# Four stacked graph-attention layers: the row of attention terms R moved by transfers instead of transposes, and a retuned list order

## The chip, the core and the metric

The kernel runs on one core of one Trainium2 chip. Time is device microseconds of one execution; a run's time is the median of several. The core has five engines that work side by side: PE (TensorE, matmuls and transposes, with PEld for its weight loads), DVE (VectorE), ACT (ScalarE), POOL (GpSimd) and SP (SyncE, which here only issues DMAs). Each engine takes its instructions in a fixed order and waits at an instruction until what it needs is there.

## What is computed

Input x has 32 batches of 512 nodes with 256 features, adj is a 512 x 512 adjacency of about 3% ones. Four layers follow one another, each on `h = relu(layernorm(x))`, each added to x:

```python
# layer 0 (layer 1 is the same with slope 0.01, relu at the end)
Wh = h @ W
e = leaky_relu((Wh @ a1)[:, :, None] + (Wh @ a2)[:, None, :], 0.2)
e = where((adj > 0) | eye(N), e, -inf)
x = x + elu(softmax(e, -1) @ Wh)
# layer 2: the same with 4 heads of 64 features
# layer 3
out = relu(h @ mlp1_w + mlp1_b)                      # 512 features
out = elu(gat(out, None, W_fc, a_fc)) + out          # attention without a mask
out = relu(out @ mlp2_w + mlp2_b)                    # 256 features
out = elu(gat(out, adj, W_hand, a_hand)) + out       # attention with the mask
x = x + relu(out)
```

All of it is in 32-bit floats.

## The kernel before

**How an attention is done.** With p the source term and q the target term of a node, exp(leaky_relu(p + q)) is a maximum of two products, so after dividing by a factor of the target row, the weight of node j for node i is `max(R[i], T[j]) * mask[j, i]` times a factor of j that is put on the values. `values` (L669) makes the tile v: for each of four tiles of 128 nodes a matmul of hT with the weights W, to which three more columns were added (W times the vectors a, with the slopes in them); ACT takes the exponential of these three columns into v[:, t, F:F+3] and scales the values by the first. `weights` (L704) makes `wt`, [j on partitions, four tiles j, 512 nodes i]: DVE's `scalar_tensor_tensor` (L714) takes the maximum of R (512 wide, the same on every partition) with a column T of v, times `maskT`. `averages` (L756) then runs the four matmuls of `wt` with v for one tile of nodes; column F of the result is the sum by which it is divided.

**Where R comes from.** R has to stand on all 128 partitions. In `weights` without `r`, PE transposes the column v[:, t, F+2], broadcast to 128 x 128, four times into a PSUM bank, and DVE reads it there. This is the way of layer 0, layer 1 and the last attention of layer 3, which all go through `plain` (L749). Layer 2 and `sort_attend` have another: `rows_out` (L721) transposes the columns once into 4 (or 16) rows of 128, ACT copies them into the SBUF tile `row` (one buffer), a DMA on SP writes them to a line in DRAM (four buffers), and `spread` (L731) reads that line back with a DMA that repeats it on 128 partitions, into a tile with three buffers.

**Streams.** Four streams each carry every fourth batch through all layers, one behind the other by LEAD. The layers are generators; each `yield after_us(t)` says when this stream goes on: the start of its last piece, plus STRETCH times the matmul time of it, plus SLOW times t. The main loop at the end of `fast` always goes on with the stream that is due first. This settles the order in which instructions are written down, and that place is their rank.

**The list scheduler.** The program is built twice. In the first pass `jobs_of` (L165) collects which instruction needs which, `price` (L110) gives each a time, and `in_order` (L251) plays them through: each engine takes, of the instructions that are ready, the one with the lowest rank. For a DMA, `price` has a landing time by kind (`spread` 4.3 us, `row` 2.6). The order of each engine and the PSUM bank of each tile are kept, and in the second pass `arrange` (L388) ties the instructions of each engine into this order. The times in `price`, LEAD, SLOW, STRETCH and the pauses thus appear in no instruction; they settle the order alone. SP's DMAs are in it as well: an SP instruction that waits for a transfer holds all that stand behind it.

**The beginning.** All loads are issued by SP in one list: two vectors for W0, x of batch 0, W0, adj, x of batches 1 to 3, then the other weights, vectors and biases. `setup` (L568), run beside the first streams with the banks of the fourth, makes the mask: DVE turns adj into ones and zeros (`own`), POOL's `affine_select` (L572) sets the diagonal to one, PE transposes it in 16 blocks, ACT copies the blocks as `maskT`. After that it finishes the weights of the later layers (`finish_w`, L498: transposes and small matmuls, POOL for the vectors, DVE for the columns) and the constants `before`, `after` and `band` for the sort.

**`sort_attend`** (L956) replaces the unmasked attention for all batches but the last: POOL scatters the rows in the order of their terms into DRAM (`order`), SP brings them back (`sums`), prefix sums are made, SP writes them as `table`, and POOL gathers from it (`g`). It stays as it is but for its pauses.

If a value is too large or adj has a case that this scheme doesn't cover, `general` computes everything again; it doesn't run with these inputs.

Of the kernel before, what the change touches and what calls it, by code (L numbers as in the profile page):

```python
# [30 lines left out]
P = 128  # L31
# [36 lines left out]
class Job:  # L68

    def __init__(self, place, ins):  # L70
        self.place, self.ins = place, ins
        self.engine, self.op = str(ins.engine).split(".")[-1], ins.opcode
        self.real, self.soft = set(), set()
        self.after, self.behind, self.opens, self.uses = [], [], [], set()
        self.ready, self.left, self.led, self.rank = 0.0, 0, False, place
# [34 lines left out]
def price(job, outs, ins, in_psum):  # L110

    e, op = job.engine, job.op
    if op == "Matmult":
        (name, _, moving), (_, _, still) = ins[0], ins[1]
        job.span = int(job.ins.tile_size[1])
        turned = name.startswith("ident")
        whole = str(list(job.ins.ins)[1].dtype).endswith("float32")
        job.passes = 2 if whole and not turned else 1
        job.rest, job.fills = [], outs[0][0]
        job.load = 109.0 * elements(still) / P * job.span / P  # L120
        job.flow = 109.0 if turned else (elements(moving) * (5.0 / 6.0 if whole else 0.45) + 2.4) * job.span / P
        return
    n = max(elements(s) for _, _, s in outs + ins) if outs + ins else 1
    wide = [name for name, _, s in ins if elements(s) > 48]
    columns = sum(1 for _, _, s in ins if elements(s) == 1) if n > 48 else 0
    if op == "DMACopy":
        name, _, s = outs[0]
        kind = name.split("_")[0].rstrip("0123456789")
        large = elements(s) * s[0][1] > 5000
        job.took = LANDING.get(kind, 6000.0) if large else SHORT.get(kind, 3300.0)  # L130
        if kind == "spread":
            job.took += 900.0 * (ins[0][1] // 512)
        if kind == "x" and ins[0][1] == 0:
            job.took = 5000.0
        job.holds = (2000.0 if kind == "order" else 1290.0) if e == "Pool" else 600.0 if kind in ("sums", "table") else 400.0
        return
    if e == "DVE":
        if op == "BNStats":
            t = 409.0
        elif n <= 48:  # L140
            t = 158.0 + n
        elif op in ("TensorTensor", "TensorReduce") or len(wide) > 1:
            t = 155.0 + 1.042 * n + (55.0 * columns if op == "TensorScalarPtr" else 0.0)
        elif any(map(in_psum, wide)):
            t = 205.0 + 1.045 * n
        else:
            t = 205.0 + 0.43 * n + 45.0 * columns
        job.holds = max(45.0, t - 84.0)
    elif e == "Activation":
        if n <= 48:  # L150
            t = 170.0 + n + 90.0 * (len(ins) > 1)
        elif any(map(in_psum, wide)):
            t = 170.0 + 0.82 * n + 90.0 * min(columns, 1)
        else:
            t = 200.0 + 0.84 * n + 85.0 * min(columns, 1)
        job.holds = max(60.0, t - 100.0)
    else:
        t = 1271.0 if op == "TensorTensor" and n > 48 else 250.0
        job.holds = t
    if len(outs) > 1:  # L160
        job.holds, t = job.holds + 85.0, t + 165.0
    job.took = t
# [88 lines left out]
def in_order(jobs, users, homes):  # L251
# [27 lines left out]
    array = {"load": 0.0, "flow": 0.0, "end": 0.0, "span": P, "idle": 0.0, "last": 0.0}  # L279
# [23 lines left out]
    def put(job, e, at):  # L303
# [21 lines left out]
        else:  # L325
            clock[e], done = at + job.holds, at + job.took
        array["last"] = max(array["last"], done)
# [71 lines left out]
def fast(ctx, tc, plan, flag, x, adj, w0, a0, w1, a1, w2, a2, mlp1_w, mlp1_b, mlp2_w, mlp2_b,  # L399
# [10 lines left out]
    LEAD = 75.63  # L410
    SLOW = 1.43
    STRETCH = 1.5
# [98 lines left out]
    a0_sb = fetch_a(a0, "W0a")  # L511
    xts = {0: load_x(0)}
    W0, _ = fetched0 = fetch_w(w0, a0_sb, "W0")
# [54 lines left out]
    def setup():  # L568
# [3 lines left out]
        nc.gpsimd.affine_select(  # L572
            out=own, in_=own, pattern=[[P, NT], [-1, N]], base=0, channel_multiplier=1,
            compare_op=OP.not_equal, fill=1.0,
        )
        nc.vector.tensor_reduce(differ[:, 0:1], adj_sb, AX.XY, OP.min)
        nc.vector.tensor_scalar(differ[:, 0:1], differ[:, 0:1], 0.0, None, op0=OP.is_lt)
        for j in range(NT):
            p = bank()
            for t in range(NT):  # L580
                transpose(p[:, t * P:(t + 1) * P], own[:, t, j * P:(j + 1) * P], ident)
            nc.scalar.copy(maskT[:, j, :], p)
        yield
# [69 lines left out]
    def turned(xn, when):  # L653
# [5 lines left out]
        yield after_us(2.12)  # L659
# [9 lines left out]
    def values(hT, w, rs=None):  # L669

        v = work.tile([P, NT, F + 3], FP, tag="v", name="v", bufs=4)
        for t in range(NT):
# [14 lines left out]
            if t + 1 < NT:  # L687
                yield after_us(0.72)
        yield after_us(0.03)
        return v  # L690

    def linear_t(inT, w, bias, name, bufs):
# [3 lines left out]
        for f in range(ft):  # L696
# [4 lines left out]
            yield after_us(0.76 if f == ft - 1 else 1.59)  # L701
# [47 lines left out]
    def plain(hT, w, rs=None):  # L749
        v = yield from values(hT, w, rs)  # L750
        wt = weights(lambda t: v[:, t, F + 2:F + 3], lambda j: v[:, j, F + 1:F + 2])
        note(v[:, :, F:])
        yield after_us(4.32)
# [19 lines left out]
    def layer0(xt, xn, rs, when):  # L773
        v, wt = yield from plain((yield from turned(xn, when)), W0)
        xn, rs = new_xn(), small([NT], "rs")
        for t0 in range(0, NT, 2):
            r, q = pair(), pair("q")
            for i in range(2):
# [3 lines left out]
                if i == 0:  # L782
                    yield after_us(2.78)
            add_elu(xt[:, t0:t0 + 2, :], r, q)
            norm(xt, xn, rs, t0, True)
            last, when = when, after_us(1.15)
            if t0 == 0:
                yield after_us(5.01)
# [3 lines left out]
    def layer1(xt, xn, rs, when):  # L792
        v, wt = yield from plain((yield from turned(xn, when)), W1, rs)
        xn, rs = new_xn(), small([NT], "rs")
        for t0 in range(0, NT, 2):
            r = pair()
            for i in range(2):
                p, rd = averages(v, wt, t0 + i)
                nc.scalar.activation(r[:, i, :], p, AF.Relu, scale=rd)
                if i == 0:  # L800
                    yield after_us(2.38)
# [3 lines left out]
            last, when = when, after_us(4.67)  # L805
            if t0 == 0:
                yield after_us(12.63)
# [3 lines left out]
    def layer2(xt, xn, rs, when):  # L811
        hT = yield from turned(xn, when)
        v = work.tile([P, NT, NH, CH], FP, tag="v", name="v2", bufs=4)
        for t in range(NT):
# [11 lines left out]
            yield after_us(0.87 if t + 1 < NT else 0.62)  # L826
# [4 lines left out]
        def begin():  # L831
# [4 lines left out]
            return after_us(1.36)  # L836
# [7 lines left out]
        yield after_us(9.98)  # L844
        begin()
        note(v.rearrange("p t h c -> p (t h) c")[:, :, D:])
        yield after_us(7.5)
        when = begin()
        for g, parts in enumerate(plan):
# [10 lines left out]
            yield after_us(0.16)  # L860
# [29 lines left out]
            yield after_us(0.3)  # L890
# [3 lines left out]
        yield after_us(9.4)  # L894
        return xn, rs, after_us(1.32)
# [28 lines left out]
    def attend(oT, b):  # L924

        halves, ends = fc_values()
        for c in range(2):
            for t in range(NT):
                project_half(oT, halves, ends, c, t)
                yield after_us(0.3)  # L930
# [4 lines left out]
        yield after_us(0)  # L935
        ys = []
        for t in range(NT):
# [10 lines left out]
            yield after_us(0.16)  # L948
            if t:
                mlp_in(oT, ys[t - 1], t - 1)  # L950
                yield after_us(0.3)
        yield after_us(3.15)
        mlp_in(oT, ys[-1], NT - 1)
        yield after_us(2.72)

    def sort_attend(oT, b):  # L956
# [6 lines left out]
        for t in range(NT):  # L963
            project_half(oT, halves, ends, 0, t)
            yield after_us(0.49)
        project_half(oT, halves, ends, 1, 0)
        yield after_us(0.06)
# [3 lines left out]
        yield after_us(0.73)  # L971
# [10 lines left out]
        sort = after_us(16.48)  # L982
        yield after_us(7.62)
        for t in range(1, NT):
            project_half(oT, halves, ends, 1, t)
            yield after_us(1.52)
# [7 lines left out]
        for c in range(2):  # L994
# [17 lines left out]
            sort = after_us(1.66)  # L1012
        places = table[:N, :].rearrange("(p t) (k c n) -> p (t k) c n", t=NT, k=2, c=2)
        sort = after_us(6.05)
        for c in range(2):
# [15 lines left out]
            yield after_us(3.52)  # L1031
# [14 lines left out]
            sort = after_us(1.5)  # L1046
        yield after_us(4.72)
# [12 lines left out]
        landed = after_us(9.21)  # L1060
        for t in range(NT):
# [13 lines left out]
            landed = after_us(2.51)  # L1075
            when.append(after_us(1.17))
# [6 lines left out]
        yield after_us(0)  # L1083

    def layer3(xt, xn, when, b):
# [3 lines left out]
        v, wt = yield from plain(rT, WHA)  # L1089

        n = 1 if b == B - 1 else 2
        for t0 in range(0, NT, n):
            y, q = pair()[:, :n, :], pair("q")[:, :n, :]
            for i in range(n):
# [3 lines left out]
                yield after_us(1.72)  # L1098
# [40 lines left out]
    def batch(b):  # L1139
        if b < NS:  # L1140
            first_norm(b)
            yield after_us(1.86)
        else:
            yield after_us(3.78)
        xt, xn, rs = normed.pop(b)
        when = after_us(4.88)
        for layer in (layer0, layer1, layer2):
            xn, rs, when = yield from layer(xt, xn, rs, when)
        if b + NS < B:
# [11 lines left out]
    ready = {i: i * LEAD + late for i, late in enumerate((0, -2.47, -0.73, -8.03))}  # L1161
    streams = [stream(i) for i in range(NS)]
    early = setup()
    ready[NS] = 0.35
    while ready:
        i = min(ready, key=ready.get)
        if i == NS:
            turn[0] = NS - 1
            ready[i] += 1.5
# [464 lines left out]
```

## Time and profile before

| | |
|---|---|
| median of 5 runs | 2784.59 us (2782.7 to 2785.1) |
| the profiled execution | 2785.95 us, from first to last instruction 2784.0 |
| mean granted TensorE clock | 0.995 |
| DMA bytes | 287.37 MB, 103 GB/s in the mean |
| DMA issues: spread, row, `sums`, `table`, out, x | 159, 63, 124, 62 + 62, 66, 32 on SP |
| DMA issues on POOL: `order`, `g` | 248, 124 |

PE's busy time is the union of its matmuls with modelled ends, so two matmuls in a row overlap by a little; the distance between their starts (the pitch) says how long each holds the array. fp32 matmuls run in two passes and count as two instructions in the trace.

### The profile page before, as it was taken

What the parts mean: (1) busy time and instruction counts of PE and PEld (TensorE: products, weight loads), DVE (VectorE), ACT (ScalarE), POOL (GpSimd) and SP (SyncE); (2) the same over time, 40 slices, a digit from 0 to 9 for tenths busy, and PEclk for the clock granted to TensorE, in tenths of its full rate; (3) what the DMA queues carried; (4) which work ended last, traced back from release to release, by engine and by line L of the source; (5) the groups of instructions that cost most, each with busy time, mean ns of one, the idle gap of its engine ahead of it and who ended that gap; (6) DMA issues with size and microseconds to landing.
All of it is one profiled execution on the core that took longest, in us unless ns stands there. A gap on an engine that the chain in (4) does not pass through costs nothing.

```text
span 2784.0 us, 41668 instructions
## 1 busy us (share of the span) xinstructions
PE 2739.4 (98%) x14316; PEld 1953.8 (70%) x14316; DVE 2272.9 (82%) x5834; ACT 1634.0 (59%) x4142; POOL 517.3 (19%) x515
## 2 busy tenths in 40 slices
PE   6999999999999999999999999999999999999997
PEld 6676686767776677766866667776686766867665
DVE  4779887897978879788796888978888898888964
ACT  3455666566655666556655566655666556655555
POOL 0012221122202222022211222111221122211220
PEclk9999999999999999999999999999999999999999
DMA  3024342343413433134331433223432233422430
GB/s 99 16 80 134 103 144 63 104 130 103 149 46 115 134 111 130 35 124 128 115 118 50 134 121 124 92 69 115 130 117 90 84 127 111 140 74 88 136 113 32
DMA packets 202499, 287.37 MB, mean 103 GB/s; under 512 B 18156, under 2 KB 157350, under 8 KB 202280
## 3 DMA queue, kind: packets, MB, share of 16 engines
q1 hardware_dynamic: 172520, 186.34, 21.5%
q0 software_dynamic: 29760, 98.30, 10.6%
q8 instruction: 114, 1.87, 0.3%
q14 instruction: 105, 0.86, 0.1%
HBM read 169.14 MB, written 115.45 MB: 102 GB/s over the span
## 4 chain that ended last, share of the span: by engine, by line
PE 92%; DVE 4%; ACT 1%; DMA 1%; issue 1%; SPq 0%; POOL 0%; POOLq 0%; ACTq 0%
PE b L430 70%; PE b L434 12%; PE b L438 10%; DVE w L714 1%; DVE st L630 0%; DVE y L771 0%; DMA W<-in_L_gnn_W_dram 0%; DVE xn L637 0%; DVE y L1107 0%; DMA spread<-row 0%; DVE y L764 0%; DMA g<-table,at 0%; DMA WHAa<-in_L_gnn_a_hand_dram 0%; DMA row<-row 0%; ACT q L780 0%
## 5 line engine op out<-in xcount | busy, mean ns | idle before, releaser
L430 PE MATMUL b<-v,w 128*128 128x257 f32 (+1 forms) x3136 | 766.0, 382 | 2.0 <-DVE w L718 1.0
L430 PEld LDWEIGHTS b<-v,w 128*128 128x128 f32 x3136 | 572.9, 191 | 122.1 <-issue 34.2
L430 PE MATMUL b<-WFC,oT 128*128 128x256 f32 (+1 forms) x2048 | 490.6, 381 | 1.5 <-ACT oT L700 1.5
L430 PEld LDWEIGHTS b<-WFC,oT 128*128 128x128 f32 x2048 | 374.4, 189 | 75.4 <-issue 18.6
L430 PE MATMUL b<-W,hT 128*128 128x259 f32 (+1 forms) x1536 | 396.0, 388 | 0.5 <-ACT hT L651 0.5
L714 DVE SCALAR_TENSOR_TENSOR w<-spread,v,maskT 128x512 f32<-128x512 f32 x512 | 373.5, 779 | 13.9 <-PE b L434 13.1
L434 PE MATMUL b<-w,v 128*32 128x512 f32 x3072 | 349.4, 595 | 0.0
L998 POOL DMA_INDIRECT order<-v,at x248 | 262.1, 1057 | 410.3 <-DVE at L980 147.0
L430 PEld LDWEIGHTS b<-W,hT 128*128 128x128 f32 x1536 | 279.0, 192 | 61.1 <-issue 22.7
L714 DVE SCALAR_TENSOR_TENSOR w<-b,v,maskT 128x512 f32<-128x512 f32 x384 | 264.7, 743 | 22.6 <-PE b L438 20.3
L1110 POOL TENSOR_TENSOR x<-x,y 128x512 f32<-128x512 f32 x62 | 81.8, 1320 | 1036.4 <-ACT y L1108 1027.1
L430 PE MATMUL b<-hT,WM 128*128 128x512 f32 x512 | 243.7, 592 | 0.4 <-ACT hT L651 0.4
L1052 POOL DMA_INDIRECT g<-table,at x124 | 137.1, 1106 | 568.0 <-DVE rden L746 180.2
L434 PEld LDWEIGHTS b<-w,v 128*32 128x32 f32 x3072 | 89.9, 109 | 198.1 <-issue 195.5
L430 PE MATMUL b<-oT,WM 128*128 128x512 f32 x512 | 227.5, 593 | 0.0
L630 DVE BATCH_NORM_STATS2 st<-x 128x6 f32<-128x256 f32 x512 | 194.4, 408 | 5.1 <-DMA x<-in_x_dram 3.7
L651 ACT ACTIVATE hT<-b 128x512 f32<-128x512 f32 x256 | 147.4, 593 | 45.6 <-PE b L438 45.6
L430 PEld LDWEIGHTS b<-oT,WM 128*128 128x128 f32 x512 | 97.2, 190 | 102.7 <-issue 99.9
L746 DVE RECIPROCAL rden<-b 128x1 f32<-128x1 f32 x388 | 57.8, 160 | 136.2 <-PE b L430 133.5
L438 PE MATMUL b<-ident,xn 128*128 128x128 f32 x1024 | 158.5, 276 | 8.2 <-DVE xn L637 8.2
L771 DVE TENSOR_TENSOR y<-q,y 128x512 f32<-128x512 f32 (+1 forms) x194 | 132.6, 683 | 33.8 <-ACT q L770 33.5
L922 ACT ACTIVATE v<-b,ends 128x256 f32<-128x256 f32 x256 | 120.4, 470 | 63.2 <-PE b L430 50.2
(154 smaller groups left out, 4236.6 us busy)
## 6 DMA issues: line engine op xcount, KB each, us to landing
table<-sums SPq DMA_DIRECT2D x62, 1032.0 KB
spread<-row SPq DMA_DIRECT2D x159, 256.0 KB
sums<-order SPq DMA_DIRECT2D x62, 516.0 KB
x<-in_x_dram SPq DMA_DIRECT2D x32, 512.0 KB
out_dram<-x SPq DMA_DIRECT2D x62, 256.0 KB
sums<-order SPq DMA_DIRECT2D x62, 129.0 KB
order<-v,at POOLq DMA_INDIRECT x248, 2.7
g<-table,at POOLq DMA_INDIRECT x124, 5.0
```

The costliest lines, as they stand in the source:

```text
L430: nc.tensor.matmul(p, w, x, **flags)
L434: nc.tensor.matmul(p, w, x, tile_position=(0, c), **flags)
L438: nc.tensor.transpose(p, x, i)
L630: nc.vector.bn_stats(st[:, i, :], xt[:, t0 + i, :])
L651: nc.scalar.activation(hT[:, :, t0 * P:(t0 + 2) * P], p.rearrange("p (k n) -> p k n", k=KF), AF.Relu)
L714: nc.vector.scalar_tensor_tensor(wt[:, j, :], r, t_col(j), maskT[:, j, :], op0=OP.max, op1=OP.mult)
L746: nc.vector.reciprocal(r, den)
L771: nc.vector.tensor_tensor(r, q, r, op=OP.add)
L922: nc.scalar.activation(halves[c][:, t, :F], ps[:, :F], AF.Copy, scale=ends[:, t, 0:1])
L998: one = nc.gpsimd.indirect_dma_start(out=orders[c], out_offset=bass.IndirectOffsetOnAxis(ap=at[:, 0, t:t + 1], axis=0), in_=halves[c][:, t ...
L1052: nc.gpsimd.indirect_dma_start(out=g, out_offset=None, in_=table, in_offset=bass.IndirectOffsetOnAxis(ap=at[:, 1, t:t + 1], axis=0),)
L1110: (nc.gpsimd if n == 2 else nc.vector).tensor_tensor(xr, xr, y, op=OP.add)
```

## The change

R of `plain` is made by `rows_out` and `spread`, as in layer 2, for layers 0 and 1 and for the last attention; the weights come after a pause of their own:

```diff
-    def plain(hT, w, rs=None):
+    def plain(hT, w, rs=None, far=False):
         v = yield from values(hT, w, rs)
-        wt = weights(lambda t: v[:, t, F + 2:F + 3], lambda j: v[:, j, F + 1:F + 2])
+        r = None
+        if far:
+            r = spread(rows_out(v[:, :, F + 2], 1)[0, :])
+            yield after_us(10.31)
+        wt = weights(lambda t: v[:, t, F + 2:F + 3], lambda j: v[:, j, F + 1:F + 2], r=r)
         note(v[:, :, F:])
-        yield after_us(4.32)
+        yield after_us(0.98)
         return v, wt
-        v, wt = yield from plain((yield from turned(xn, when)), W0)
+        v, wt = yield from plain((yield from turned(xn, when)), W0, far=True)
-        v, wt = yield from plain((yield from turned(xn, when)), W1, rs)
+        v, wt = yield from plain((yield from turned(xn, when)), W1, rs, far=True)
-        v, wt = yield from plain(rT, WHA)
+        v, wt = yield from plain(rT, WHA, far=True)
```

The diagonal of the mask is set by DVE after the transposes, and the loads of W0's two vectors go behind W0:

```diff
         nc.vector.tensor_scalar(own, adj_sb, 0.0, None, op0=OP.is_gt)
-        nc.gpsimd.affine_select(
-            out=own, in_=own, pattern=[[P, NT], [-1, N]], base=0, channel_multiplier=1,
-            compare_op=OP.not_equal, fill=1.0,
-        )
...
             nc.scalar.copy(maskT[:, j, :], p)
+            nc.vector.tensor_tensor(maskT[:, j, j * P:(j + 1) * P], p[:, j * P:(j + 1) * P], ident, op=OP.max)
...
-    a0_sb = fetch_a(a0, "W0a")
     xts = {0: load_x(0)}
-    W0, _ = fetched0 = fetch_w(w0, a0_sb, "W0")
+    W0, _ = fetched0 = fetch_w(w0, a0, "W0")
```

In the planner, loads from the inputs (but not those of x from batch 4 on) count one behind the other, and a transpose counts as one of the full array, whatever its width:

```diff
         turned = name.startswith("ident")
+        job.span = P if turned else int(job.ins.tile_size[1])
...
-        if kind == "x" and ins[0][1] == 0:
-            job.took = 5000.0
+        if ins[0][0].startswith("in_") and not (kind == "x" and ins[0][1] >= 4 * 512 * 256):
+            job.took, job.flux = 2500.0, max(160.0, 4.0 * elements(s) * s[0][1] / 350.0)
...
+            if job.flux:
+                done = array["pipe"] = max(done, array["pipe"]) + job.flux
```

All pauses get other values (some forty numbers in `after_us`; only a few are shown), and the first batch of each stream gets one more after each of its first three layers:

```diff
-    LEAD = 75.63
-    SLOW = 1.43
-    STRETCH = 1.5
+    LEAD = 81.65
+    GO = 7.0
+    PAUSES = (11.15, 4.8, 0, 9.84, 8.43, 1.6, 8.25, 7.21, 13.16, 3, 15.72, 19.74)
+    SLOW = 1.52
+    STRETCH = 1.8
...
-        for layer in (layer0, layer1, layer2):
+        for i, layer in enumerate((layer0, layer1, layer2)):
             xn, rs, when = yield from layer(xt, xn, rs, when)
+            if b < NS:
+                yield after_us(PAUSES[3 * b + i])
...
-    ready = {i: i * LEAD + late for i, late in enumerate((0, -2.47, -0.73, -8.03))}
+    ready = {i: i * LEAD + late for i, late in enumerate((0, 3.23, 4.34, 10.53))}
...
-    ready[NS] = 0.35
+    ready[NS] = 0.04
...
-            ready[i] += 1.5
+            ready[i] += 11.92
```

`GO` is used nowhere.

## The prediction

> **What bounds the kernel now.** I read the page's first part, then the stretches, then PE's waits.
>
> ```profile
> span 2784.0 us, 41668 instructions
> PE 2739.4 (98%) x14316; PEld 1953.8 (70%) x14316; DVE 2272.9 (82%) x5834; ACT 1634.0 (59%) x4142; POOL 517.3 (19%) x515
> ```
> ```profile
> 0.00:100.00 100.00, 75.82 (x374) 64.80 (x375) 51.37 (x161) 39.54 (x110) 5.72 (x18) 0.91 0.26 77
> 442.00:779.00 337.00, 336.84 (x1770) 239.81 (x1769) 284.03 (x728) 203.19 (x516) 66.23 (x64) 1.00 0.34 108
> 779.00:1116.00 337.00, 336.84 (x1769) 239.95 (x1768) 283.91 (x729) 203.27 (x516) 65.55 (x64) 1.00 0.34 108
> 2466.00:2784.00 318.00, 299.72 (x1485) 209.79 (x1483) 227.67 (x556) 173.57 (x424) 50.72 (x51) 0.99 0.26 84
> ```
> The columns after the stretch and its length are busy us of PE, PEld, DVE, ACT and POOL, then granted clock, DMA share and GB/s. The work repeats every 337.1 us (one batch of each of the four streams; the same long PE pieces in the chain that ended last start at 442.47, 779.59 and 1116.71). In such a round PE is idle 0.2 us and DVE has 53 us to spare. All of PE's 36 us of idle time lie at the two ends: 24 in the first 100 us, 10 in the last. So one us of PE work taken out of a round is one us off the round, as long as PE then waits for nothing new. The early waits by name (total, times, longest):
>
> ```profile
> PE b L438 <- DVE xn L637: 8.2, 11, 3.8
> PE b L438 <- POOL own L572: 4.2, 1, 4.2
> PE b L438 <- DVE W L487: 3.3, 1, 3.3
> ```
>
> **The change: what PE no longer does.** For layers 0 and 1 and the last attention, `weights` turned a broadcast column into R with four transposes; now one transpose turns the four columns into rows (`rows_out`), and two DMAs (row to DRAM, row spread to 128 partitions) do the rest.
>
> ```profile
> L438 PE MATMUL b<-ident,v 128*128 128x128 f32 x384 | 67.8, 276 | 0.0
> L714 DVE SCALAR_TENSOR_TENSOR w<-spread,v,maskT 128x512 f32<-128x512 f32 x512 | 373.5, 779 | 13.9 <-PE b L434 13.1 <-DMA spread<-row 0.7
> L714 DVE SCALAR_TENSOR_TENSOR w<-b,v,maskT 128x512 f32<-128x512 f32 x384 | 264.7, 743 | 22.6 <-PE b L438 20.3 <-PE b L434 1.8
> ```
> ```profile
> 1023.98 0.60 PE L438 MATMUL b<-ident,v 128*128 128x128 f32 x4
> 1024.42 0.60 PE L438 MATMUL b<-ident,rT 128*128 128x128 f32 x4
> 1032.25 0.27 PE L438 MATMUL b<-ident,ends 128*4 128x128 f32 x1
> 1032.36 1.90 PE L430 MATMUL b<-v,w 128*128 128x257 f32 x8
> ```
> The 67.8 us busy overlap with neighbours; what counts is the pitch. Four transposes hold the array from 1023.98 to 1024.42, so 0.109 us each, and the narrow one of `ends` 0.11. Removed: 384 x 0.109 = 41.9 us. Added: 32 batches x 3 = 96 narrow ones x 0.109 = 10.5. Net -31.4 us, 3.9 a round.
>
> **What goes onto other engines.** ACT gets 96 copies of a 4-row tile (0.24 us each at 1032.88), 23 us on an engine at 59%. DVE's 384 products read R from SBUF instead of PSUM. Their mean would rise from 743 to 779 ns, but the medians of both forms are 743 (the SBUF form has stragglers up to 2147), so between 0 and 14 us more, at most 1.7 a round against 53 spare: nothing on the path. Were that cover gone, it would cost those 14. [...]
>
> SP issues 192 more DMAs, each spread waiting at the queue's head for its row. The wait of spreads for rows was 109.1 us over 63, so 1.7 us; with the two issues (0.27 and 0.34) a round gets 12 x 2.3 = 28 us of SP, whose long waits are for ACT's rows (525 us), that is, it is usually there first. Behind a blocked SP stand `sums<-order`, table writes and output; their consumers waited little (DVE for g 4.1 us in all). DMA bytes: 96 x 256 KB = 25 MB on 287, share 0.34 to about 0.37. POOL loses only the diagonal fill of the mask; SP's order of loads changes only in W0 going ahead of its two vectors.
>
> **What becomes late: the trip of R.** Formerly DVE could start 0.5 us after PE's transposes. Two trips where the wait was for the transfer itself:
>
> ```profile
> 158.69 0.27 PE L438 MATMUL b<-ident,ends 128*4 128x128 f32 x1
> 159.61 0.27 SPq L728 DMA_DIRECT2D row<-row  x1
> 160.84 0.33 SPq L734 DMA_DIRECT2D spread<-row  x1
> 164.56 0.75 DVE L976 SCALAR_TENSOR_TENSOR junk<-spread,ends,band 128x512 bf16<-128x512 f32 x1
> ```
> ```profile
> 1033.14 0.26 SPq L728 DMA_DIRECT2D row<-row  x1
> 1036.30 0.34 SPq L734 DMA_DIRECT2D spread<-row  x1
> 1040.41 0.75 DVE L976 SCALAR_TENSOR_TENSOR junk<-spread,ends,band 128x512 bf16<-128x512 f32 x1 [0.19 <-DMA spread<-row]
> ```
> So 5.9 us from transpose to first use in a quiet stretch, 8.2 (from 1032.25) in a loaded one. PE then needs the first product (0.75) and, since four products take 2.7 us and the first three matmul pairs only 3 x 0.435, about 0.75 more: trip + 1.5, that is 7.4 to 9.7 us of other PE work as cover. The changed program's PE order gives this cover directly. I added the pitches (0.109 a transpose, 0.435 a 257-column pair, 0.855 a 512-column one, 0.224 a 32-column one) between each narrow transpose and the first matmul on its weights. From the second round on the twelve covers of a round are 9.0, 11.8, 10.4, 9.4, 10.4, 12.2, 10.1, 9.8, 10.1, 9.4, 9.5 and 9.3 us. At 7.4 nothing waits. At 9.7 five of them are short, by 0.7, 0.3, 0.3, 0.2 and 0.4: 1.9 us a round, 15 in eight rounds. Between 0 and 15 I take 4: of the 63 old trips' DMA packets in the trace, the middle one had landed 5.9 us after its transpose, and one in ten later than 8.4. The last two covers at the end are 7.1 and 8.0: 0 to 2.6 us each, taken as 0.
>
> **The beginning.** There the covers are 3.4, 4.0, 3.6 and 8.3 us, since few streams run. First R: SP can't issue its row before the list of loads is through; the last of them was issued at 27.80 to 28.20. From row issue to first use took 4.95 us (159.61 to 164.56) to 7.27, so the product starts at 33.2 to 35.5 and the first matmul at 33.9 to 36.2, where it stood at 33.00 before. By then PE has done 11.6 us of work by pitch instead of 9.9. Net -0.8 to +1.5, taken +0.5. The 4.2 us for POOL's fill of `own` and the 3.3 for DVE (which sat behind POOL's `ties`) vanish from their places, but go into this wait: what they won is given back here. If it is not given back, 7.5 less. The mask's four small products cost DVE 4 x 0.285 (nearest row: L880, 128x128, 285 ns), before R lands. Second R: 7.4 - 4.0 = +3.4. Third: its 3.6 and that wait, 7.0, so +0.4. After such a pause the clock falls:
>
> ```profile
> 30.00:35.00 5.00, 4.51 (x18) 4.07 (x19) 3.34 (x11) 0.74 (x2) 0.00 (x0) 0.52 0.25 88
> 35.00:40.00 5.00, 5.00 (x29) 4.69 (x30) 0.50 (x3) 1.55 (x3) 0.00 (x0) 0.80 0.02 3
> ```
> After the 3.3 us wait these ten us lost 5 x 0.48 + 5 x 0.20 = 3.4 us, so the second wait may cost 0 to 3.4 more; I take 1.5. [...]
>
> The altered pauses, LEAD, SLOW, STRETCH and the planner's prices issue nothing; they only move the order, which the covers already contain.
>
> **Sum.** Against the profiled execution (2785.95, span 2784.0): -31.4 + 0.5 + 3.4 + 0.4 + 1.5 + 4 = -21.6, so 2764.3. That execution was 1.36 above the median of 2784.59; forecast **2763**. Own range: 2745 (no new waits but the second R's, and the 7.5 kept) to 2777 (15 steady, 3.4 clock, 1.5 and 2 at the ends).
>
> **Rivals.**
> - *Trips too long for their covers (slower).* Place: the eight repeating rounds. With a trip T the shortfalls are T + 1.5 minus each cover. At T = 8.55 they add up to 3.9 us a round, exactly the gain; above it the change loses. At 9.4 (one use stood at 298.01 after its transpose at 288.63) they are 11.6 a round, 93 in all; if two neighbours share a wait, half: 2785 - 31 + 46 + 6 = **2805**. For it: 12 more trips a round lengthen SP's and the DMA queues, and the 1032 trip was at 8.2. Against: the middle trip at 5.9.
> - *DVE takes over.* It holds 284 of 337 us now, 286 of 333 then. It would need stretches where it is behind; if half the gain goes there, **2774**. Against: PE waited for DVE's products 0.7 us in the whole run.
> - *Nothing arrives:* the early waits and clock eat the gain, 2779 to 2790, say **2784**. Against: they are paid once, the gain eight times.
>
> **How the numbers follow.** Forecast 0.70, DVE 0.06, nothing 0.06, slower 0.15, and 0.03 for less than 2745 (the ends' 36 us of idle time shrink too). Predicted 2763. The range 2745 to 2784 leaves out the slower case, the 0.03 and little else. A measurement of this kernel tells 0.2% (5.6 us) from no change: faster 0.79, same 0.06, slower 0.15.
>
> **What would show it.** Right: the 384 wide transposes gone, rounds of 333 to 335 us, PE waiting for L714 by under 2 us a round, the first product near 34 us. Wrong: rounds at or above 337 with PE idle behind L714 or spreads (the slower rival), or PE idle behind DVE without a transfer in the chain.

## The result, and the profile after

The changed kernel takes **2790.17 us** (median of 21 runs, 2787.66 to 2794.01) where the kernel before took 2784.64 in the same runs (41 runs, 2782.03 to 2788.75): ratio **1.0019** [1.0013, 1.0025]. It is slower by 0.2%, 27 us away from the forecast of 2763. The profiled execution took 2788.22, its span 2786.2.

The first part of the page of the changed kernel, and its stretches (columns as before: busy us of PE, PEld, DVE, ACT and POOL, then granted clock, DMA share, GB/s):

```profile
span 2786.2 us, 41640 instructions
PE 2715.8 (97%) x14028; PEld 1918.0 (69%) x14028; DVE 2264.9 (81%) x5838; ACT 1638.5 (59%) x4238; POOL 530.9 (19%) x514
```
```profile
0.00:100.00 100.00, 77.21 (x380) 61.35 (x384) 55.01 (x171) 41.44 (x121) 3.85 (x17) 0.90 0.30 88
442.00:779.00 337.00, 333.24 (x1730) 235.24 (x1729) 282.69 (x728) 202.87 (x528) 66.86 (x64) 1.00 0.38 117
779.00:1116.00 337.00, 333.59 (x1733) 235.94 (x1732) 282.80 (x728) 203.58 (x528) 68.39 (x64) 1.00 0.38 117
2466.00:2784.00 318.00, 301.89 (x1494) 211.11 (x1492) 232.09 (x563) 180.27 (x441) 56.62 (x54) 0.99 0.31 97
```
PE has 23.6 us less to do, and the span is 2.2 us longer. The beginning isn't where it went: the first 100 us have 22.8 us of idle PE, and had 24.2. It is the repeating rounds. PE's idle time in 337 us was 0.2 and is now 3.4 to 3.8. I take a round's length from one mark that every round has (the matmuls from `hT` with `WM`, 64 to a round); the mean of five rounds in the middle was 337.4 us and is 337.9. The work that was taken out has come back as waiting, with the clock at 1.00.

Whom PE and DVE wait for from 450 to 2450 us, some six rounds (us in total, times, longest). For PE:

```profile
PE b L442 <- ACT y L863: 9.9, 12, 1.3
PE b L434 <- DVE w L714: 6.7, 6, 1.9
PE b L442 <- DVE y L775: 2.2, 6, 0.4
PE b L442 <- DVE xn L637: 1.9, 6, 0.3
PE b L442 <- ACT y L1101: 1.8, 4, 0.7
```
For DVE:

```profile
DVE w L714 <- DMA spread<-row: 33.3, 23, 3.4
```
And the group of the weights' products over the whole run, which had 0.7 us of waiting for spreads before:

```profile
L714 DVE SCALAR_TENSOR_TENSOR w<-spread,v,maskT 128x512 f32<-128x512 f32 x896 | 652.2, 762 | 51.7 <-DMA spread<-row 51.2
```
PE's longest list is not behind L714 but behind ScalarE's copy `y4` of layer 2 (L863) and other small things, none of which touches a transfer. The wait for a transfer sits one engine further back: DVE stands 33.3 us for spreads, and what is queued behind it on DVE, then ACT, reaches PE late.

Here is such a place in the timeline of the changed kernel (start, length, engine, line, operation; in brackets the idle time before and what ended it). First a plain layer's trip:

```profile
1690.68 0.27 PE L442 MATMUL b<-ident,v 128*4 128x128 f32 x1
1691.29 0.56 SPq L1048 DMA_DIRECT2D table<-sums  x1
1691.39 0.24 ACT L726 COPY row<-b 4x128 f32<-4x128 f32 x1
1691.93 0.51 SPq L728 DMA_DIRECT2D row<-row  x1
1697.00 0.34 SPq L734 DMA_DIRECT2D spread<-row  x1
1700.07 2.08 DVE L714 SCALAR_TENSOR_TENSOR w<-spread,v,maskT 128x512 f32<-128x512 f32 x3 [1.50 <-DMA spread<-row]
1700.87 0.70 PE L434 MATMUL b<-v,w 128*128 128x257 f32 x2 [0.78 <-DVE w L714]
```
A row of 2 KB, issued 0.64 us behind a table write of 1 MB, needs 5.1 us until SP can issue the spread. Now the four spreads of layer 2, which the kernel before had too; first SP's rows of the timeline, then DVE's:

```profile
1620.29 0.56 SPq L1048 DMA_DIRECT2D table<-sums  x1
1620.90 3.02 SPq L734 DMA_DIRECT2D spread<-row  x3
```
```profile
1627.87 1.41 DVE L714 SCALAR_TENSOR_TENSOR w<-spread,v,maskT 128x512 f32<-128x512 f32 x2 [3.44 <-DMA spread<-row]
```
The first of them is issued 0.61 us behind a table write, and DVE, whose next instruction in order is the product that reads it, stands for 3.44 us. PE's waits of 0.35 to 1.29 us at L863, L1101 and L775 follow between 1634 and 1658. Of the 32 first spreads of layer 2, 7 stand so, 0.61 to 0.63 us behind a write, and land 6.4 to 6.9 us after their issue; DVE's waits at these 7 make up all of its 21.4 us for layer 2. In the kernel before, no write went out in the 5.4 us ahead of any of them, and they landed after 3.0 to 4.0 us.

Sorted by what SP had issued from 4 us before the row up to the spread, the 96 new trips of the changed kernel read as follows (medians, us). The third column runs from the end of the row's issue to the start of the spread's, so it also holds what SP issues between the two. The fourth runs from the end of the spread's issue to its last packet, and slack from there to the first use:

| ahead of the spread on SP | trips | row issued to spread issued | spread issued to last packet | whole trip | slack |
|---|---|---|---|---|---|
| nothing large | 50 | 1.42 | 2.57 | 5.39 | 1.57 |
| other large transfers | 14 | 2.39 | 2.56 | 6.33 | 0.89 |
| a 1 MB table write | 32 | 2.40 | 4.12 | 8.45 | 0.37 |

A slack of 0.37 is the handover alone (where DVE stood waiting for the spread, the product began 0.30 to 0.63 us after the last packet): the trips behind a table write are those that are waited for. These 32 are of two kinds. In 14 the write was issued ahead of the row; from the start of its issue to its landing, as its semaphore tells it, the row then takes 4.42 us and the spread 3.24. In the other 18 the write was issued between row and spread; the row takes 1.15 us and the spread 5.82. With no write in the 8 us ahead it is 1.16 and 3.22. So a write delays whichever of the two follows it.

### The profile page after: what moved, and what is told of

Same layout as the page of the kernel before. It is cut to its first block, busy times and chain, and to the rows that moved or that the text cites. A ratio compares the mean times of both kernels' runs of the same rounds, so it can differ in the third digit from the quotient of the medians.

```text
span 2786.2 us, 41640 instructions
## 1 busy us (share of the span) xinstructions
PE 2715.8 (97%) x14028; PEld 1918.0 (69%) x14028; DVE 2264.9 (81%) x5838; ACT 1638.5 (59%) x4238; POOL 530.9 (19%) x514
## 4 chain that ended last, share of the span: by engine, by line
PE 69%; DVE 20%; DMA 5%; ACT 3%; issue 2%; SPq 1%; DVEq 0%; ACTq 0%
PE b L434 55%; PE b L438 8%; PE b L442 6%; DVE w L714 6%; DMA spread<-row 3%; DVE st L630 2%; DVE y L775 2%; DMA row<-row 1%; DVE sums L1047 1%; DVE xn L641 1%; DVE y L1111 1%; DVE sums L1032 1%; DVE q L773 1%; DVE y L768 1%; DVE x L769 1%
## 5 line engine op out<-in xcount | busy, mean ns | idle before, releaser
L434 PE MATMUL b<-v,w 128*128 128x257 f32 (+1 forms) x3136 | 751.4, 382 | 19.8 <-DVE w L714 17.7
L714 DVE SCALAR_TENSOR_TENSOR w<-spread,v,maskT 128x512 f32<-128x512 f32 x896 | 652.2, 762 | 51.7 <-DMA spread<-row 51.2
L434 PE MATMUL b<-WFC,oT 128*128 128x256 f32 (+1 forms) x2048 | 500.3, 381 | 0.0
L434 PE MATMUL b<-W,hT 128*128 128x259 f32 (+1 forms) x1536 | 378.9, 387 | 1.4 <-ACT hT L651 1.0
L775 DVE TENSOR_TENSOR y<-q,y 128x512 f32<-128x512 f32 (+1 forms) x194 | 135.9, 700 | 53.2 <-ACT q L774 39.6
L442 PEld LDWEIGHTS b<-ident,xn 128*128 128x128 f32 x1024 | 123.8, 142 | 67.1 <-issue 26.1
L442 PE MATMUL b<-ident,y 128*128 128x128 f32 x896 | 133.9, 275 | 19.5 <-ACT y L863 11.2
L774 ACT ACTIVATE q<-q,minus 128x512 f32<-128x512 f32 (+1 forms) x194 | 138.3, 713 | 11.0 <-DVE q L773 8.2
```

The costliest lines, as they stand in the source:

```text
L434: nc.tensor.matmul(p, w, x, **flags)
L442: nc.tensor.transpose(p, x, i)
L714: nc.vector.scalar_tensor_tensor(wt[:, j, :], r, t_col(j), maskT[:, j, :], op0=OP.max, op1=OP.mult)
L774: nc.scalar.activation(q, q, AF.Exp, bias=minus1)
L775: nc.vector.tensor_tensor(r, q, r, op=OP.add)
```

## The experiments

Each run was timed beside the kernel before, and ratios are against that. E3 and E4 plan the order anew. In all others every instruction of TensorE, VectorE and GpSimd keeps its place in the order (E12 adds some to GpSimd's); a changed operand or another issuing engine is put in after planning (`plan` is set in the second pass). Line numbers of an edited kernel stand up to 15 lower down. E8 and E9 of this list ran on a chip on which the kernel before takes 2817.18; there only ratios compare.

**E1: the spread doesn't wait for the row.**

```diff
-            r = spread(rows_out(v[:, :, F + 2], 1)[0, :])
+            line = rows_out(v[:, :, F + 2], 1)[0, :]
+            r = spread(x[0, 0:2, :].rearrange("t f -> (t f)") if plan else line)
```


> The changed kernel with the same order on every engine, but the 96 spreads of the three new places read 512 numbers of x in DRAM instead of the row that was just written, so they no longer wait for the row's landing (the rows are still written, the same bytes move; the attention terms R of these three layers are wrong). Theory T (the new trips are too long for their covers, above all where the row's small DMA queues behind a large one, 5.1 us at 1691.93): a trip loses the 1.3 to 5.3 us from row issue to spread issue, most of the 4 us a round come back, 2762 to 2770. Rival O (the retuned order itself places copies and products late, for instance PE's wait for the copy of L863, 1.3 us a round): R is not what is waited for, 2784 to 2791.

2783.34 us, ratio 0.9996 [0.9987, 1.0006]: just under the rival's side, and far from theory T's. PE's wait behind L714 fell from 6.7 to 0.6 us in the six rounds, that behind L863 stayed (9.8). DVE still waited 44.4 us for spreads: 24.1 of it for layer 2's, which the edit leaves alone, and 19.8 for the plain layers', which had been 30.1. Taking the row out of the chain is not enough, for the spread itself still stands behind the table write (the 32 that do took 6.11 us in the median).

**E2: the plain layers' products wait for no trip.**

```diff
             r = spread(rows_out(v[:, :, F + 2], 1)[0, :])
+            if plan:
+                r = WM1[:, 0, :]
```


> Same order again; rows and spreads of the three new places are issued as before and land, but their products read a constant tile in SBUF instead of the spread one, so nothing waits for the trip at all (R of these layers is a constant, the output is wrong). Theory T: all waits that the trip made are gone, 2755 to 2763. Rival O: 2782 to 2790, the waits at the copies remain.

2771.27 us, ratio 0.9955 [0.9938, 0.9972]; round 336.7. Between the two expectations: the new trips are worth 0.64% (1.0019 less 0.9955, 18 us), and yet 3 us of idle PE a round stay, half of them behind L863, as in the changed kernel. DVE's wait for spreads was 23.9 us, all of it layer 2's.

**E3: the transfers undone, all else as changed.**

```diff
-        v, wt = yield from plain((yield from turned(xn, when)), W0, far=True)
+        v, wt = yield from plain((yield from turned(xn, when)), W0)
...
-        v, wt = yield from plain((yield from turned(xn, when)), W1, rs, far=True)
+        v, wt = yield from plain((yield from turned(xn, when)), W1, rs)
...
-        v, wt = yield from plain(rT, WHA, far=True)
+        v, wt = yield from plain(rT, WHA)
```


> The changed kernel with R of the three layers by transposes again, all else kept (its pauses, planner, mask, loads); the order is planned anew. PE has 31.4 us more work, SP 192 DMAs fewer. Theory T: the 31 us of work replace about 30 us of waits, 2780 to 2796. Rival O: the order's own waits stay and the work is added, 2810 to 2820.

2807.60 us, ratio 1.0088 [1.0072, 1.0105], round 340.1: between the two expectations, nearer the rival's. Under the changed pauses and prices the transfers gain 17 us; all the rest without the transfers loses 23 against the kernel before. They were chosen together, so this doesn't say what the mask or the load order is worth alone.

**E4: the planner is told that a row takes 2 us longer.**

```diff
-SHORT = {"table": 5200.0, "row": 2600.0, "out": 4500.0}
+SHORT = {"table": 5200.0, "row": 4600.0, "out": 4500.0}
```


> The changed kernel with one number of its planner altered: a row counts as landed 4.6 us after its issue instead of 2.6, so products and matmuls of R are placed later (PE's covers go from 9.0 to 12.2 a round to 9.4 to 16.9, mostly over 11.5). Theory T: waits behind R shrink to under 1 us a round, 2763 to 2775. Rival O: a new order of the same kind, 2782 to 2796.

2849.39 us, ratio 1.0240 [1.0223, 1.0257], far outside both. The longer covers on PE didn't help; DVE's waiting for spreads doubled:

```profile
L714 DVE SCALAR_TENSOR_TENSOR w<-spread,v,maskT 128x512 f32<-128x512 f32 x896 | 644.7, 755 | 106.2 <-DMA spread<-row 104.1 <-PE b L438 1.9 <-issue 0.2
```
In the new order 37 of the 96 trips have a table write ahead, and the 31 of them with nothing else large took 10.58 us. The planner prices a row and a spread by their own size, whatever stands ahead of them, so a better figure for the row does not steer around the write.

**E5: as E2, and layer 2's products wait for no trip either** (`known` is the pass's `plan`, a name that layer 2 uses for something else).

```diff
-                weights(lambda t: v[:, t, h, D + 2:D + 3], lambda j: v[:, j, h, D + 1:D + 2], r=far[h])
+                weights(lambda t: v[:, t, h, D + 2:D + 3], lambda j: v[:, j, h, D + 1:D + 2], r=WM1[:, 0, :] if known else far[h])
```


> The instructions of every engine stand in the changed kernel's order. Beside the products of the three plain layers, those of layer 2 read a constant row in place of their spread (the computation is changed there, and nothing waits for a spread of layers 0 to 3 any more; the trips themselves are still made). Theory T2 (the 3 us a round that stayed when only the plain layers' products were freed come from layer 2's spreads, which stand behind a 1 MB table write on SP's queue and hold DVE 3.4 us a round): TensorE's waits on the copies of line 863 fall to the 1 us that the kernel before had, the round goes to 333.5 to 334.5, the time to 2745-2757. Theory O (the new order itself puts copies and sums late): DVE's 20 us go away and TensorE's waits stay, 2766-2773.

2750.01 us, ratio 0.9870 [0.9854, 0.9887]; round 333.7. Its stretches, and PE's waits from 450 to 2450:

```profile
0.00:100.00 100.00, 82.27 (x427) 62.45 (x427) 57.67 (x177) 42.95 (x125) 3.88 (x17) 0.93 0.31 90
442.00:779.00 337.00, 336.25 (x1753) 239.28 (x1752) 285.62 (x734) 206.15 (x535) 66.93 (x64) 1.00 0.38 117
```
```profile
PE b L443 <- DVE xn L638: 1.9, 6, 0.3
PE b L443 <- ACT y L866: 0.8, 5, 0.2
PE b L435 <- ACT hT L652: 0.2, 1, 0.2
```
T2 holds, O falls. The wait behind ScalarE's copy, 9.9 us in the changed kernel, is 0.8 once DVE doesn't stand at layer 2's spreads, though no instruction of the three engines has moved. All the trips still run here, and their bytes (DMA share 0.38): what costs is waiting for them.

**E6: the table writes are issued by ScalarE.**

```diff
     order, array = in_order(jobs, users, homes)
+    for job in list(order["SP"]):
+        name, _, steps = view([a for a in job.ins.outs if hasattr(a, "bass_ap")][0])
+        if name.startswith("table") and elements(steps) * steps[0][1] > 5000:
+            order["SP"].remove(job)
+            line = order["Activation"]
+            line.insert(sum(1 for other in line if other.at <= job.at), job)
...
-            nc.sync.dma_start(places[:, :, c, :], flat[c])
+            (nc.scalar if plan else nc.sync).dma_start(places[:, :, c, :], flat[c])
```
The planned order is left alone; only these 62 writes are taken out of SP's list and put into ScalarE's at their planned time.

> Planned order unchanged on TensorE, VectorE and GpSimd; only the 62 table writes of 1 MB leave SP's queue and are issued by ScalarE at the place in its order that the plan's time gives. Theory Q (a small row or spread is slow because it is queued behind the 1 MB write: in the changed kernel the 32 trips of the plain layers with such a write ahead take 8.45 us from transpose to landing, the 50 with nothing ahead 5.39): the 32 come down to 5.5-6.5, VectorE's waits for spreads from 51.7 us to under 20, the time to 2768-2779. Rival (the write takes the same 16 DMA engines whoever issues it, and the small packets wait for these): trips stay at 8 us, waits over 40, 2785-2795. [...]

2767.92 us, ratio **0.9931** [0.9915, 0.9948], round 335.8. The time is theory Q's, at its lower end. The group of products and PE's steady waits (450 to 2450) in this run:

```profile
L720 DVE SCALAR_TENSOR_TENSOR w<-spread,v,maskT 128x512 f32<-128x512 f32 x896 | 651.4, 760 | 15.6 <-DMA spread<-row 14.7 <-issue 0.2
```
```profile
PE b L448 <- ACT y L869: 7.4, 7, 1.3
PE b L448 <- DVE xn L643: 3.2, 8, 0.7
PE b L448 <- DVE y L781: 2.0, 4, 0.6
```
The same trips in both kernels, those that had a table write ahead on SP in the changed one (medians, us, columns as above):

| | row to spread issue, changed | row to spread issue, E6 | spread to last packet, changed | spread to last packet, E6 | whole, changed | whole, E6 |
|---|---|---|---|---|---|---|
| 32 of the plain layers | 2.40 | 1.31 | 4.12 | 4.39 | 8.45 | 8.09 |
| 8 of layer 2 (first head) | 2.27 | 1.34 | 5.14 | 2.75 | 9.81 | 6.20 |

DVE's wait for layer 2's spreads fell from 21.4 to 0.9 us, for the plain layers' from 30.1 to 14.4. But the trips of the plain layers were expected at 5.5 to 6.5 us and are at 8.1, as the rival had them. What the moved write changes is who goes first:

```profile
1611.53 8.64 SPq L740 DMA_DIRECT2D spread<-row  x4
1611.88 0.53 ACTq L1054 DMA_DIRECT2D table<-sums  x1
```
In the changed kernel SP had issued the write 0.61 us ahead of seven of these eight spreads of layer 2. In E6 ScalarE issues it 0.04 to 0.47 us behind them, and from issue to landing they take 3.82 us in place of 6.65. Where the write kept its lead, the other queue won little or nothing: seven plain spreads have it 2.02 us ahead in both kernels and take 5.62 and 5.57 us; eight rows have it 1.34 and 1.42 us ahead and take 4.34 and 4.07. The fall from 2.40 to 1.31 is no quicker row (1.17 and 1.16 us to its landing, in the median of the 32). It is in good part SP, which in 18 of them issues the spread 0.39 us after the row's landing in place of 1.02.

PE's wait behind layer 2's copy (L869 here, 7.4 us) is nearly that of the changed kernel (9.9), though layer 2's spreads are hardly waited for any more. DVE now waits for the rows `g` that GpSimd gathers from the table, 0.7 us in these rounds of the changed kernel:

```profile
DVE g L1076 <- DMA g<-table,at: 8.0, 12, 1.6
```
In the round that I followed, DVE stands 1.62 us for `g` at 957 and PE 1.29 us behind the copy at 976; in the changed kernel's same round DVE stands 2.87 us for the spread and PE 1.29 behind the same copy. So a part of what E6 wins at the spreads it loses again at the table's readers.

**E7: the rows, not the writes, by ScalarE.**

```diff
-        nc.sync.dma_start(row_d.rearrange("n (t p) -> t n p", p=P), row)
+        (nc.scalar if plan else nc.sync).dma_start(row_d.rearrange("n (t p) -> t n p", p=P), row)
```


> Planned order unchanged on TensorE, VectorE and GpSimd; only the 159 small rows (4 to 16 packets of 512 bytes) are issued by ScalarE, which copied them, at the plan's time; the spreads and the table writes stay on SP. Theory Q: a row no longer stands behind the table write (landing 1.4 us, not 2.4 with a write near), but the spread still may, and layer 2's four do: half of the gain of the run that moves the table writes, 2776-2785. Rival (the engines, not the queue): 2786-2794.

2789.85 us, ratio 1.0012 [1.0002, 1.0022]: the rival's side, and nothing of the half that theory Q expected. DVE waited 46.3 us for spreads. A row that ScalarE issued behind SP's write still took 4.15 us to land: a queue of its own didn't free it.

**E8: the writes and the rows by ScalarE** (both edits).

> Planned order unchanged on TensorE, VectorE and GpSimd; the 62 table writes and the 159 small rows both go by ScalarE at the plan's times, only the spreads (and the reads) stay with SP. The run with the table writes alone gave 2767.9, the one with the rows alone 2789.9. Theory Q (what counts is who stands behind a 1 MB write on one issuing engine's queue): here the rows stand behind it again, on ScalarE's queue, and the spreads do not: between the two, 2768-2778, rows landing 2.2-2.6 us where a write is near, as in the changed kernel. Rival (the moved writes helped because SP's own instruction stream got shorter, not by the queue of transfers): the stream gets shorter still, 2762-2768.

2798.79 us where the kernel before took 2817.18, ratio 0.9933 [0.9919, 0.9948]. That is E6's ratio. It makes 2766 us of the 2784.6 of the other chips, in the rival's range, and the interval (2762 to 2770) reaches into theory Q's, so the time doesn't tell them apart. It does show that 159 issues fewer on SP add nothing to what the 62 moved writes give. The four runs together show what a queue of its own is worth. Here are the transfers of the plain layers whose issue began 0.5 to 2.1 us after that of a write (median us from the start of the issue to the landing, in brackets how many):

| issued by | rows behind a write | spreads behind a write |
|---|---|---|
| all by SP (changed kernel) | 4.42 (14) | 5.82 (18) |
| writes by ScalarE (E6) | 4.07 (8) | 6.06 (21) |
| rows by ScalarE (E7) | 4.15 (14) | 6.01 (18) |
| writes and rows by ScalarE (E8) | 4.08 (14) | 5.89 (15) |
| no write in the 8 us ahead (changed kernel) | 1.16 (75) | 3.22 (58) |

Behind a write a transfer is slow, whether it stands on the write's queue or on another: the queue that theory Q named is not the cause.

**E9: E6, and the first three trips (planned before 60 us), rows and spreads, by ScalarE.**

```diff
-        if name.startswith("table") and elements(steps) * steps[0][1] > 5000:
+        if name.startswith("table") and elements(steps) * steps[0][1] > 5000 or name.startswith(("row", "spread")) and job.at < 60000.0:
```


> The run with the table writes by ScalarE, and beside them the first three trips of R (rows and spreads planned before 60 us) by ScalarE too; planned order unchanged on TensorE, VectorE and GpSimd. In the changed kernel the first row was copied by ScalarE at 20.4 us, but SP, which was still issuing the loads of weights one by one, issued it at 28.3 and its spread at 31.7, and TensorE stood 6.1 us for the first weighted sum. Theory (SP's in-order issue of the loads holds the first trip): TensorE's wait falls to 0-2 us, the time to 2761-2765. Rival (the row then waits for the loads' bytes in the transfer engines, or ScalarE, which now waits for the row to land before it can issue the spread, holds up its own copies): 2766-2772.

2785.88 against 2817.18, ratio **0.9896** [0.9883, 0.9910], the best of those that leave nothing out; by this ratio some 2756 us on the chip of the others (0.9896 x 2784.6). The first trip in the changed kernel (the instructions on tile `row` from 14 to 40 us: count, shortest, middle and longest duration in ns, first and last start; then who waited for it, us and times):

```profile
L726 ACT COPY row<-b x1: 250/250/250, 20.4 to 20.4; 4x128 f32<-4x128 f32 x1
L728 SPq DMA_DIRECT2D row<-row x1: 340/340/340, 28.3 to 28.3; - x1
...
  DVE w L714: 6.0, 1
```
and in this run:

```profile
L741 ACT COPY row<-b x1: 249/249/249, 22.7 to 22.7; 4x128 f32<-4x128 f32 x1
L743 ACTq DMA_DIRECT2D row<-row x1: 518/518/518, 23.0 to 23.0; - x1
L749 ACTq DMA_DIRECT2D spread<-row x1: 414/414/414, 27.1 to 27.1; - x1
...
  DVE w L729: 0.3, 1
```
The row lay ready at 20.7 us, and SP came to it 7.6 us later, since it issues the list of loads one by one. Issued by ScalarE it is not held up, and DVE's wait falls from 6.0 to 0.3 us. The gain over E6 (0.35%, 10 us) is larger than the 3 to 7 us that its expectation meant, but the two ran on different chips, and what goes beyond 7 is not explained.

**E10: the kernel before, its table writes by ScalarE.**

> The kernel before, its plan unchanged, with its 62 table writes of 1 MB issued by ScalarE. Its VectorE waited only 0.7 us for spreads in the whole run, so theory Q expects nothing here: 2782-2787. If the time falls below 2780, the moved write is worth something for a reason that has nothing to do with the rows.

2798.93 us, ratio 1.0045 [1.0029, 1.0062]; round 339.5. Neither expectation: it loses 13 us. PE's waits behind DVE's `y` (L777 here, L771 in the kernel before) rose from 6.1 to 13.8 us. So the moved write is no gain of itself. What rose with it is DVE's wait for the gathered rows `g`, from 4.1 to 28.4 us in the whole run:

```profile
DVE g L1072 <- DMA g<-table,at: 28.4, 15, 2.6
```
ScalarE issues a write as soon after its sums as SP did (0.08 and 0.07 us in the median), so it is not a late issue; why the gathered rows come late stays open.

**E11: E6 once more, on a further chip.**

> The run with only the table writes by ScalarE once more, on the same chip as the one above, since the run with the early trips as well was made on another chip (the kernel before at 2817.2 there): ratio 0.993 again, by 0.9915-0.9948 of the first run. If it comes to 0.990 or less here, the early trips were not worth the 0.35% between the two runs.

2768.18 us, ratio 0.9929 [0.9916, 0.9943]. E6 stands.

**E12: as E9, but the table writes by GpSimd.**

```diff
-            (nc.scalar if plan else nc.sync).dma_start(places[:, :, c, :], flat[c])
+            (nc.gpsimd if plan else nc.sync).dma_start(places[:, :, c, :], flat[c])
```


> As the run with the first three trips by ScalarE, but the 62 table writes of 1 MB are issued by GpSimd at the plan's times, not by ScalarE, whose queue held each for 0.52 us (32 us in all). Planned order of TensorE and VectorE unchanged. Theory Q (any queue but SP's will do): rows and spreads as quick as in that run, VectorE's waits for spreads under 12 us, and ScalarE's 32 us free: ratio 0.986-0.990. Rival (GpSimd's issue is slow, and the gathers and additions behind the waiting write come late): 0.991-1.000.

2777.53 us, ratio 0.9972 [0.9960, 0.9984]: faster than the kernel before, and worse than E9 by the rival's side. Each issue took 0.89 us on GpSimd, and GpSimd stood 218 us for DVE's sums ahead of the writes (L1063, the line of the write):

```profile
POOL table L1063 <- DVE sums L1055: 218.2, 21, 15.0
```
DVE's wait for spreads was 15.7 us, three times E9's 5.3. Which of the two made up the difference stays open.

## Why the prediction was wrong

**What PE no longer does** (-31.4): right. With all waiting for trips gone (E5) PE is busy 2706.2 us, 33.2 fewer than before, and the round is 333.7, inside the 333 to 335 that I had named as the sign. In the changed kernel the busy time shows only 23.6 less; that the other 9.6 come back because PE is fed piecemeal is argued, not shown.

**The beginning** (+5.8 in four terms): too dark, not the cause. The first weighted sum began at 35.56 us, where I had put it between 33.9 and 36.2, after a wait of 6.1. The second wait was 1.4 and not 3.4, and a third over 0.5 us didn't come. The waits for GpSimd's `own` (4.2) and for `W` (3.3) are gone from the list; I had said they would be given back in full. In idle time the first 100 us ended 1.4 us better than before. As to the clock: PE was granted 0.50 from 25 to 35 us, in the second half of which it did nothing, then 0.58 from 35 to 40, then 1.00.

**SP "is usually there first"**: wrong where it mattered. I averaged SP's waits over the run and looked at who waits for what stands behind a blocked SP. I didn't ask what goes out just *ahead* of the row or the spread: SP issues it at once, and the transfer then runs beside 1 MB that started earlier. A third of the trips had a write there, 8.45 us against 5.39.

**PE's idle time** of "36 us" was read too low: 2784.0 less 2739.4 is 44.6 us, 24 in the first 100 us and 18 in the last 318. The sum doesn't use it.

**Steady waits at the new trips** ("Between 0 and 15 I take 4"): the size was low, inside its bounds. From E2 to the changed kernel a round grows from 336.7 to 337.9, 1.2 us, so 10 in eight rounds.

**The step that failed** is "The altered pauses, LEAD, SLOW, STRETCH and the planner's prices issue nothing; they only move the order, which the covers already contain", together with "nothing on the path" for DVE. My covers were counted for the three plain layers and on PE's order alone. Layer 2's trips, unchanged in number, were not in them. Their spreads had cost DVE 0.7 us in the whole run with the old order; the new order issues 7 of the 32 first ones 0.61 us behind a table write and lets DVE come to them at once: 21.4 us of waiting, and from E5 to E2 a round grows by 3.1 us, from 333.7 to 336.7. That is 24 us in eight rounds, a term which my sum did not have. DVE's 53 us to spare in a round were no cover for it: DVE works in order, and while it stands at the head of its queue, the sums that would have released ScalarE's copies and PE's transposes stand behind it (with DVE's wait gone in E5, PE's wait behind the copy was 0.8 us in place of 9.9).

The ledger in spans of the profiled executions: 2784.0 before; with no wait for any trip 2747.2 (E5, -36.8); with layer 2's waits 2767.0 (E2, +19.8); with the plain layers' as well 2786.2 (+19.2, of which 10 steady and the rest at the two ends). By the ratios of the timed runs the last two steps are 24 and 18 us. My sum had 9.8 for the plain layers' trips (4 steady, 5.8 at the beginning) and nothing for layer 2's.

**The rivals.** "Trips too long for their covers" had the side right and half of the mechanism: a third of the trips did take 8.45 us, near its point of 8.55. Its place was PE behind L714, and PE waited only 6.7 us there in six rounds. "DVE takes over" asked for DVE's load, which had no part in it (283 us of 337). What came was between the two: DVE idle, holding others up. "Nothing arrives" named 2779 to 2790, and 2790.17 came, but not by its way: the beginning ended 1.4 us better, and it was the rounds that lost.

**The queue.** I then took SP's queue for the cause of the slow transfers (theory Q), and the runs don't bear it out: by E6 to E8 a transfer behind a write is about as slow on another queue. Layer 2's spreads became quicker in E6 because SP no longer issues a write ahead of them (3.82 us from issue to landing in place of 6.65). Behind a write on the same queue a row took 4.42 us and a spread 5.82, behind one on another queue 4.07 and 6.06 (E6). Why a transfer is slow there was not shown.

## What to carry to other kernels

When an operation is replaced by a round trip through memory, look at which large transfers are issued just ahead of it, by any engine, not only at the trip's length when quiet: here a 1 MB write ahead made 5.4 us into 8.5, and moving the write to another engine helped where it then went out behind the trip (3.82 us in place of 6.65 for layer 2's spreads). Count cover on the engine that reads the result, in its own order, for every transfer of this kind that the new order moves, the old ones too; here DVE's 53 us to spare in a round hid nothing of what stood behind its waiting head, and 21.4 us of waiting cost 24. And test such a suspicion with the order held fixed: a planner run anew with one altered price cost 59 us more by itself.

## What the runs showed of the hardware

A 2 KB row landed 1.16 us after the start of its issue with no 1 MB write in the 8 us ahead, and 4.42 us behind one (up to 5.05); a 256 KB spread took 3.22 and 5.82 (up to 6.92). With write and transfer issued by different engines it was 4.07 to 4.15 for the rows and 5.89 to 6.06 for the spreads. Issuing the 1 MB write holds the issuing engine's queue for 0.56 us on SP, 0.52 on ScalarE and 0.89 on GpSimd. Two chips differed by 1.2% for one kernel (2784.6 and 2817.2), and E6 had the same ratio on two chips (0.9931 and 0.9929).
